# The output projection of six of eight sequences as seven products of 128x128 blocks, its matrix read by groups from memory

## The chip, the core and the metric

The program runs on one core of a Trainium2 chip, alone. The metric is device time in microseconds (us). Names used below: PE is the matrix engine (its weight loads, which run beside the products, are listed as PEld), DVE the vector engine, ACT the scalar engine, POOL the GpSimd engine, SP the engine that only issues transfers. A transfer (DMA) is issued by SP, ACT or POOL and carried out by sixteen DMA engines that all of them share. SBUF is the memory that the engines work on, PSUM the one that PE writes to; both have 128 partitions.

## What is computed

One transformer block over 8 sequences of 512 rows, 256 wide: attention with 16 query heads in 4 groups (each group has one key and one value head), then a mixture of 64 experts (six for each row) with a shared expert. Cut to what matters here:

```python
q = (x @ wq + bq).reshape(b, t, G, QPG, D).transpose(0, 2, 3, 1, 4)   # G=4 groups, QPG=4 heads each, D=128
k, v = (kv[..., :D], kv[..., D:])
scores = einsum('bgqtd,bgksd->bgqts', q + pe, k + pe) / sqrt(D)       # causal, softmax -> probs
out = einsum('bgqts,bgksd->btgqd', probs, v).reshape(b, t, G * QPG * D)
return out @ wo                                                       # 512 x 2048 times 2048 x 256 per sequence
...
x = x + layernorm(attention(layernorm(x)))
x = x + layernorm(experts(layernorm(x)))
```

The change is about the line `out @ wo`. All data are float32.

## The kernel before

The order of all instructions on every engine is written out by hand; nothing is moved by a scheduler. One loop runs over k = 0 .. 127: eight sequences b, sixteen steps s in each (k = 16 b + s). A step has one quarter of the rows of one group of heads: `scores(k, q)` for four q (products `psc`, L507; DVE masks them and takes the least, L511; ACT takes the exponential, L515), `weigh(k)` (POOL divides by the sum, tile `e`, L525), `turned(k)` (DVE turns 32x32 blocks into `eb`, L543; SP writes `eb` to memory `ex_d` in four transfers, L547, and reads it back as `et` in one, L553) and `mix(k)` (products `pav` of `et` with the values, L580; ACT adds a bias and leaves the result `ao`, L591). They are staggered: step k of the loop holds `scores(k)`, `weigh(k)`, `turned(k - 1)` and `mix(k - 2)`. A step's data therefore leave SBUF and come back while PE works on the two following steps, and this order, together with the one queue of SP, sets when `et` is there.

Two steps make a half j = k // 2 of a group: four heads, two row tiles of 128. `project(j, i)` multiplies one tile's four heads with the group's 4 x 128 rows of `wo` into one PSUM bank pair `po` (tags o0 and o1), which adds up over the four groups of a sequence. It runs two halves later: `projections(k)` handles half k // 2 - 2, one tile in the even step and the other in the odd one. The whole matrix, `wo_sb` (2 MB), stays in SBUF. After a sequence's last half ACT copies the sums out (`copies`, L1026), in step s = 2 of the next sequence; layer norm, gate and experts of that sequence follow in later steps (`feed_forward`, places such as "5B" or "6M" in the step).

Where DVE, ACT or POOL have work of a sequence's feed forward, steps are longer; a step takes 6.2 to 9 us where there is little of it (s = 14, 15, 0 to 5), about 8 to 14 us elsewhere, and 14 to 23 us late in the run, where the experts' weights are loaded (ACT's queue) and multiplied.

The queries are already made in a similar way: `ask` and `answer` (L411) form each pair of heads from seven products of summed blocks instead of eight.

Of the kernel before, what the change touches and what calls it, by code (L numbers as in the profile page):

```python
# [19 lines left out]
P = 128  # L20
B, T, E = 8, 512, 256
NT = B * T
NI = T // P
# [18 lines left out]
LROW = ROW + NX  # L42
TH = T // 2
JOINED_FROM, JOINED_TO = 2, (EARLY + 1) * G

@with_exitstack
def sandwich_kernel(ctx, tc, x, wq, bq_t, wkv, bk_t, bv, wo, gate_wt, w_gate, w_up, w_down,
# [19 lines left out]
    y_d = dram.tile([2 * (ET_ROWS + CAP), E], F32, tag="y_d", name="y_d")  # L67
    lxg_d = dram.tile([NT - ET_ROWS, LROW], F32, tag="lxg_d", name="lxg_d")
    ly_d = dram.tile([NT - ET_ROWS, E], F32, tag="ly_d", name="ly_d")

    def bank(shape, name):
        return ps_m.tile(shape, F32, tag="m", name=name)
# [80 lines left out]
    with ExitStack() as part:  # L153
# [13 lines left out]
        def load(ap, shape, name):  # L167
            t = wpool.tile(shape, F32, tag=name, name=name)
            nc.sync.dma_start(out=t, in_=ap)
            return t  # L170
# [18 lines left out]
        for c in range(NC):  # L189
# [6 lines left out]
        bv_sb = load(bv.rearrange("(g d) -> d g", d=D), [D, G], "bv_sb")  # L196
        wq_sb = [wq_first] + [load(wq[:, ts(g, QPG * D)].rearrange("(c p) n -> p c n", p=P), [P, NC, QPG * D],
                                   f"wq_sb{g}") for g in range(1, G)]
        wo_sb = load(wo.rearrange("(h d) e -> d h e", d=D), [D, NH, E], "wo_sb")

        sg_sb, su_sb = [wpool.tile([P, NC, FSH + NX // 2], F32, tag=name, name=name) for name in ("sg_sb", "su_sb")]
        for half, (t, w) in enumerate(((sg_sb, sh_gate_t), (su_sb, sh_up_t))):
# [315 lines left out]
        def weigh(k):  # L518
            l = live[k]
            recip = small.tile([P, NI], F32, tag="recip", name=f"recip_{k}")  # L520
            nc.vector.reciprocal(recip, l["total"])  # L521
            engine = nc.gpsimd if k < NK - 1 else nc.vector
            for q in range(NI):
                e = blocks_of(k, q)
                engine.tensor_scalar(e, e, recip[:, q : q + 1], 1.0, ALU.mult, ALU.mult)  # L525
# [45 lines left out]
        def mix(k):  # L571
            b, g, m, _ = units_of(k)
            et = live.pop(k)["et"]

            pav = [bank([P, QPG, 2, HALF], f"pav_{k}")] * 2
            if k == NK - 1:
                pav[1] = bank([P, QPG, 2, HALF], f"pav_{k}_1")
            for n, _, first, count in placed(k):
                for j in range(count):
                    nc.tensor.matmul(pav[n // NI][:, :, n % 2, :], lhsT=seqs[b]["v"][g][:, j, :], rhs=et[:, :, first + j, :],  # L580
                                     start=j == 0, stop=j == count - 1, skip_group_check=True)
            if k % 2 == 0:
                results[k // 2] = {i: p2.tile([D, QPG, P], F32, tag="ao", name=f"ao_{k}_{i}", bufs=3)
                                   for i in tiles_at(k // 2)}
            bias = bv_sb[:, g : g + 1]
            for n, _, _, _ in placed(k):
                ao = results[k // 2][n // 2][:, :, ts(n % 2, HALF)]
                if k == NK - 1 and n < NI:
                    nc.vector.tensor_scalar_add(ao, pav[n // NI][:, :, n % 2, :], bias)
                else:  # L590
                    nc.scalar.activation(ao, pav[n // NI][:, :, n % 2, :], AF.Identity, bias=bias)  # L591
# [3 lines left out]
        def tiles_at(j):  # L595

            return (1, 2) if j % 2 else (0, 3)

        def project(j, i):
            b, n = divmod(j, 2 * G)  # L600
            if n == 0 and i == 0:
                po[b] = [ps_o.tile([P, 2, E], F32, tag=f"o{n}", name=f"po_{b}_{n}") for n in range(2)]
            ao = results[j].pop(i)
            for h in range(QPG):
                nc.tensor.matmul(po[b][i // 2][:, i % 2, :], lhsT=ao[:, h, :], rhs=wo_sb[:, n // 2 * QPG + h, :],  # L605
                                 start=n == 0 and h == 0, stop=n // 2 == G - 1 and h == QPG - 1, skip_group_check=True)

        def projections(k):

            j, odd = divmod(k, 2)  # L610
            j -= 2
            if j < 0:
                return
            if j % (2 * G) == 2 * G - 1:
                tiles = () if odd else tiles_at(j)
            else:
                tiles = tiles_at(j)[odd : odd + 1]
            for i in tiles:
                project(j, i)

# [394 lines left out]
        def feed_forward(b):  # L1017


            xt, sums = seqs[b]["x"], po.pop(b)  # L1020
            l = {}

            def copies():
                l["o"] = p1.tile([P, NI, E], F32, tag="xn", name=f"o_{b}")
                for n in range(2):
                    nc.scalar.copy(l["o"][:, ts(n, 2), :], sums[n])  # L1026
# [223 lines left out]
        queries(1)  # L1250
        values(0, 0, 0)
        values(0, 0, 1)
        behind, ahead = {}, iter(())
        routed, zeroing = experts(), zeros()
        twice, finishing = False, 0
        FIRST_FREE = (EARLY + 1) * NH + 6
# [4 lines left out]
        for k in range(NK):  # L1261
# [7 lines left out]
            if s == 6 and b <= EARLY:  # L1269
                ahead = prepare(b + 1)  # L1270
                next_rows.append(next(ahead))
            if 0 <= k - 1 < NK - 2:
                turned(k - 1)
            if twice and not finishing:
# [14 lines left out]
            if k < 2:  # L1289
                queries(k + 2)  # L1290
            weigh(k)
            if b <= EARLY and s == 7:
                next(ahead)()
            side(s, "A")
# [23 lines left out]
            if k == 2:  # L1318
                group_step(2)
                group_step(3)  # L1320
            if k >= 2:
                mix(k - 2)
            if in_pairs(k - 1):
# [20 lines left out]
                load_down("late")  # L1344
            if s == 2 and b:
                behind = feed_forward(b - 1)
            side(s, "D")
            if s == 6 and b == EARLY + 1:
                ahead = prepare(b + 1)
# [108 lines left out]
```

## Time and profile before

| | |
|---|---|
| median of three runs | 1357.95 us (1354.87 to 1360.82) |
| time of the profiled execution | 1357.09 us |
| its span, first to last instruction | 1355.4 us |
| instructions | 20372 |
| PE, PEld | 98 %, 75 % of the span |
| DVE, ACT, POOL | 65 %, 40 %, 34 % |
| granted PE clock | 0.996 |
| DMA | 261.32 MB, mean 193 GB/s |

A share is busy time over the span. Durations of products in the profile overlap, since products are pipelined: what a product costs PE is the distance from its start to the next one's start, read from a timeline. A float32 product shows as two rows (two instructions), so that `project` has 1024 rows for 512 products. A transfer's row gives only the time that its engine needs to issue it; when it landed is seen from who waits for it.

### The profile page before, as it was taken

Reading aid. Unit: us, or ns where it says so; the run is one execution under the profiler, and the core shown is the slowest. Engines: PE = TensorE matmul, PEld = TensorE weight load, DVE = VectorE, ACT = ScalarE, POOL = GpSimd, SP = SyncE. Lnnn points to the kernel's source line nnn. Section 1 sums busy time; section 2 is a strip of 40 time slices with the busy share of each in tenths; the row PEclk is TensorE's granted clock in tenths of the full one; section 3 lists DMA queues with packets and bytes.
Section 4 is the critical chain, followed back from the end, with each engine's and each line's share of the span. In section 5 each row is a group of like instructions: output and inputs, shape, how many; then the busy total and the mean of one; then the engine's idle time right before and its main releaser. Section 6 shows DMA issues by size and latency. Waiting matters only on the chain. (4 is left out here: it accounts for less than half of the span.)

```text
span 1355.4 us, 20372 instructions
## 1 busy us (share of the span) xinstructions
PE 1333.5 (98%) x6266; PEld 1015.5 (75%) x6266; DVE 879.9 (65%) x2871; ACT 543.7 (40%) x1655; POOL 460.8 (34%) x772
## 2 busy tenths in 40 slices
PE   9999999999999999999999999999999999999997
PEld 6888777788778887788778877876666766767774
DVE  5575577766776677667786678657666444567545
ACT  3343354334443444334433443334433343434423
POOL 4334232313231242223221232134554444445511
PEclk9999999999999999999999999999999999999999
DMA  8676667655674576466665556569998889777712
GB/s 266 175 201 172 192 195 207 158 154 159 209 186 132 151 218 189 118 171 174 201 166 152 156 171 183 151 194 292 304 268 258 244 255 291 182 238 227 244 36 71
DMA packets 167388, 261.32 MB, mean 193 GB/s; under 512 B 17756, under 2 KB 141629, under 8 KB 167277
## 3 DMA queue, kind: packets, MB, share of 16 engines
q1 hardware_dynamic: 129117, 206.76, 52.9%
q10 hardware_dynamic: 32016, 43.78, 10.4%
q0 software_dynamic: 6144, 9.44, 3.6%
q8 instruction: 51, 0.84, 0.3%
q14 instruction: 60, 0.49, 0.1%
HBM read 147.99 MB, written 111.94 MB: 192 GB/s over the span
## 5 line engine op out<-in xcount | busy, mean ns | idle before, releaser
L525 POOL TENSOR_SCALAR e<-e,recip 128x512 f32<-128x512 f32 (+1 forms) x504 | 245.8, 527 | 684.2 <-DVE recip L521 543.2
L515 ACT ACTIVATE e<-e,least 128x32 f32<-128x32 f32 (+1 forms) x504 | 259.4, 517 | 259.2 <-DVE least L511 242.6
L580 PE MATMUL pav<-et,v 128*128 128x256 f32 x1280 | 301.5, 383 | 8.4 <-DMA et<-ex_d 7.6
L580 PEld LDWEIGHTS pav<-et,v 128*128 128x128 f32 x1280 | 243.2, 191 | 48.4 <-DMA et<-ex_d 7.5
L511 DVE CUSTOM_DVE_ANT_0 e<-psc,mask 128x32 f32<-128x32 f32 (+1 forms) x504 | 203.8, 430 | 111.7 <-PE psc L507 109.7
L507 PE MATMUL psc<-kt,qt 128*128 128x32 f32 (+15 forms) x1024 | 275.5, 407 | 0.8 <-DVE qt L372 0.4
L591 ACT ACTIVATE ao<-pav,bv_sb 128x256 f32<-128x256 f32 x255 | 107.2, 471 | 379.3 <-PE pav L580 356.5
L605 PE MATMUL po<-wo_sb,ao 128*128 128x256 f32 x1024 | 241.9, 380 | 0.0
L605 PEld LDWEIGHTS po<-wo_sb,ao 128*128 128x128 f32 x1024 | 193.3, 190 | 51.3 <-issue 16.6
L507 PEld LDWEIGHTS psc<-kt,qt 128*128 128x128 f32 x1024 | 161.1, 191 | 60.4 <-DVE least L511 26.0
L543 DVE STREAM_TRANSPOSE eb<-e 128x1024 f32<-128x1024 f32 (+1 forms) x252 | 197.5, 822 | 2.1 <-POOL e L525 1.5
L515 ACT ACTIVATION_READ_ACCUMULATOR e<-e,least 128x1 f32 x504 | 95.5, 190 | 0.0
L848 POOL DMA_INDIRECT y_d<-dd,idx x32 | 50.9, 1589 | 91.2 <-DMA y_d<-dd,idx 27.0
L367 PE MATMUL pq<-xnt,wq_sb 128*128 128x256 f32 x320 | 75.5, 380 | 0.2 <-DMA wq_sb<-in_wq 0.2
L320 DVE SCALAR_TENSOR_TENSOR kt<-pk,bk_sb,pe_sb 128x512 f32<-128x512 f32 x32 | 24.0, 750 | 76.6 <-PE pk L318 73.9
L411 PE MATMUL pq_back<-rows_joined,heads 128*128 128x256 f32 x264 | 71.3, 379 | 0.0
L329 PEld LDWEIGHTS pv<-wkv_sb,xnt 128*128 128x128 f32 x512 | 65.9, 192 | 4.5 <-issue 1.1
L329 PE MATMUL pv<-wkv_sb,xnt 128*128 128x128 f32 x512 | 67.5, 275 | 0.5 <-ACT ao L591 0.5
L367 PEld LDWEIGHTS pq<-xnt,wq_sb 128*128 128x128 f32 x320 | 59.5, 190 | 9.8 <-DMA wq_sb<-in_wq 1.1
L411 PEld LDWEIGHTS pq_back<-rows_joined,heads 128*128 128x128 f32 x264 | 50.2, 190 | 16.2 <-issue 8.2
L318 PE MATMUL pk<-xnt,wkv_sb 128*128 128x512 f32 x128 | 60.5, 595 | 0.4 <-DMA wkv_sb<-in_wkv 0.4
L120 DVE COPY ht<-pth 88x256 f32<-88x256 f32 x32 | 13.4, 419 | 63.3 <-PE pth L828 58.5
(237 smaller groups left out, 1534.4 us busy)
## 6 DMA issues: line engine op xcount, KB each, us to landing
ex_d<-eb SPq DMA_DIRECT2D x504, 160.0 KB
et<-ex_d SPq DMA_DIRECT2D x126, 640.0 KB
wgu<-in_w_gate ACTq DMA_DIRECT2D x32, 352.0 KB
wgu<-in_w_up ACTq DMA_DIRECT2D x32, 352.0 KB
wd<-in_w_down ACTq DMA_DIRECT2D x32, 352.0 KB
y<-y_d ACTq DMA_DIRECT2D x10, 512.0 KB
x<-in_x SPq DMA_DIRECT2D x7, 512.0 KB
out_dram<-x SPq DMA_DIRECT2D x7, 512.0 KB
```

Of the source, the lines that this page charges most:

```text
L318: nc.tensor.matmul(pk, lhsT=wkv_sb[:, c, g, 0, :], rhs=s["xnt"][:, c, :], start=c == 0, stop=c == NC - 1)
L329: nc.tensor.matmul(pv[:, i, :], lhsT=s["xnt"][:, c, ts(2 * n + i, P)], rhs=wkv_sb[:, c, g, 1, :], start=c == 0, stop=c == NC - 1, skip_gro ...
L367: nc.tensor.matmul(pq[:, n, :, :], lhsT=wq_sb[g][:, c, ts(2 * pair + n, D)], rhs=seqs[b]["xnt"][:, c, :].rearrange("p (u v) -> p u v", v=P ...
L411: nc.tensor.matmul(out, lhsT=factor[0], rhs=factor[1], start=first, stop=last, skip_group_check=True)
L507: nc.tensor.matmul(psc[:, :w], lhsT=halves[k // 2][:, at, :, :].rearrange("d h t -> d (h t)"), rhs=seqs[b]["kt"][g][:, :w], start=True, st ...
L511: nc.vector.tensor_tensor_reduce(out=e, in0=psc[:, :w].rearrange("p (c t) -> p c t", t=BS), in1=mask[:, T - w :].rearrange("p (c t) -> p c ...
L515: nc.scalar.activation(e, e, AF.Exp, bias=l["least"][:, q : q + 1], scale=-1.0, accum_out=l["total"][:, q : q + 1])
L525: engine.tensor_scalar(e, e, recip[:, q : q + 1], 1.0, ALU.mult, ALU.mult)
L543: nc.vector.transpose(eb[:, :, first : first + count, :, :].rearrange("p a j r t -> p j a r t"), weighed[k % 2][:, end - count : end, :, : ...
L580: nc.tensor.matmul(pav[n // NI][:, :, n % 2, :], lhsT=seqs[b]["v"][g][:, j, :], rhs=et[:, :, first + j, :], start=j == 0, stop=j == count ...
L591: nc.scalar.activation(ao, pav[n // NI][:, :, n % 2, :], AF.Identity, bias=bias)
L605: nc.tensor.matmul(po[b][i // 2][:, i % 2, :], lhsT=ao[:, h, :], rhs=wo_sb[:, n // 2 * QPG + h, :], start=n == 0 and h == 0, stop=n // 2 = ...
```

## The change

For sequences 1 to 6 (`CROSSED`) the projection of one half, a 2 x 2 problem of blocks (two row tiles, two pairs of heads, two halves of the 256 columns, each block pair twice for n = 0, 1), is made from seven products of blocks instead of eight. PE has 14 products of 128x128x128 per half instead of 8 of 128x128x256.

- `cross(j)` forms four sums of blocks of `ao` on POOL, at the head of the even step. `straight(j)` (6 products, bank o0) stands in the even step, `across(j)` (8 products, bank o1) in the odd one; for the last half of a sequence both are in the even step.
- The banks no longer add up over the groups. `add_up` adds each bank to `partial` in SBUF: ACT copies it for the first two halves, DVE adds it (`tensor_add`) for the other six. `combine` (POOL, six instructions) makes the two row tiles' outputs from the seven sums, twice a sequence; ACT's `copies` goes.
- `wo_sb` goes. `load_whole(n)` reads one group's 512 KB in ACT's queue (sequences 0 and 7, and the first in the prologue). While sequence 0 is worked on, `make_sets` forms each group's seven blocks on POOL and writes them to memory; in sequences 1 to 6 `load_sets` reads them back in ACT's queue, 384 KB (`ws`) in steps with k % 4 = 3 and 512 KB (`wc`) in steps with k % 4 = 0, one buffer each, after the exponentials of that step.
- `ao` has one buffer of both tiles instead of three of one tile, so ACT may write the next half only when `cross` and `straight` have read the last. In sequences 0 and 7 both tiles are projected in the even step.

```diff
+CROSSED = range(1, B - 1)
-        wo_sb = load(wo.rearrange("(h d) e -> d h e", d=D), [D, NH, E], "wo_sb")
+        def load_whole(n):
+            t = whole[n] = wpool.tile([D, QPG, E], F32, tag="wc", name=f"wo_{n}")
+            nc.scalar.dma_start(out=t, in_=wo.rearrange("(h d) e -> d h e", d=D)[:, ts(n % G, QPG), :])
+        load_whole(0)
+        partial = wpool.tile([P, 2, 7, P], F32, tag="partial", name="partial")
...
+        def make_sets(g):
+            w = blocks_of_whole(whole[g])
+            t = p1.tile([P, 4, 2, P], F32, tag="xt2", name=f"sets_{g}")
+            for k in range(2):
+                nc.scalar.dma_start(out=ws_d[g][:, k], in_=w[:, k, 0])
+            nc.scalar.dma_start(out=wc_d[g][:, 0], in_=w[:, 1, 1])
+            nc.gpsimd.tensor_sub(t[:, 0], w[:, 0, 1], w[:, 0, 0])
+            nc.gpsimd.tensor_sub(t[:, 1], w[:, 1, 1], t[:, 0])
+            yield
+            nc.gpsimd.tensor_sub(t[:, 2], w[:, 1, 1], w[:, 0, 1])
+            nc.gpsimd.tensor_sub(t[:, 3], w[:, 1, 0], t[:, 1])
+            yield
+            nc.scalar.dma_start(out=wc_d[g][:, 1:], in_=t[:, :3])
+            nc.scalar.dma_start(out=ws_d[g][:, 2], in_=t[:, 3])
+            yield
+        def load_set(n, d, name):
+            t = wpool.tile(list(d[0].shape), F32, tag=name, name=f"{name}_{n}")
+            nc.scalar.dma_start(out=t.rearrange("p k n e -> p (k n e)"), in_=d[n % G].rearrange("p k n e -> p (k n e)"))
+        def cross(j):
+            x11, x12, x21, x22 = sides_of_results(j)
+            t = crossed[j] = p2.tile([D, 4, 2, P], F32, tag="ac", name=f"crossed_{j}", bufs=1)
+            nc.gpsimd.tensor_add(t[:, 1], x21, x22)
+            nc.gpsimd.tensor_sub(t[:, 2], t[:, 1], x11)
+            nc.gpsimd.tensor_sub(t[:, 3], x11, x21)
+            nc.gpsimd.tensor_sub(t[:, 0], x12, t[:, 2])
+        def straight(j):
+            x11, x12, _, x22 = sides_of_results(j)
+            w = sets[j // 2]["ws"]
+            po[j, 0] = multiply(j, [[(x[:, n], w[:, k, n]) for k, x in enumerate((x11, x12, x22))] for n in range(2)],
+                                "ps", "o0")
+        def across(j):
+            w, t = sets[j // 2]["wc"], crossed.pop(j)
+            po[j, 1] = multiply(j, [[(t[:, k, n], w[:, k, n]) for k in range(4)] for n in range(2)], "pc", "o1")
+        def add_up(j, part):
+            ...
+            if n < 2:
+                on_act(sums, bank_)
+            else:
+                nc.vector.tensor_add(sums, bank_, sums)
+        def combine(b, odd):
+            ...
+            nc.gpsimd.tensor_add(first[:, 0], t[:, 0], t[:, 1])
+            nc.gpsimd.tensor_add(t[:, 5], t[:, 0], t[:, 5])
+            nc.gpsimd.tensor_add(t[:, 6], t[:, 5], t[:, 6])
+            nc.gpsimd.tensor_add(t[:, 3], t[:, 4], t[:, 3])
+            nc.gpsimd.tensor_add(second, t[:, 2:5:2], t[:, 6:7].to_broadcast([P, 2, P]))
+            nc.gpsimd.tensor_add(first[:, 1], t[:, 5], t[:, 3])
...
             if k % 2 == 0:
-                results[k // 2] = {i: p2.tile([D, QPG, P], F32, tag="ao", name=f"ao_{k}_{i}", bufs=3)
-                                   for i in tiles_at(k // 2)}
+                tag = "ac" if b == B - 1 and k % 4 else "ao"
+                results[k // 2] = p2.tile([D, 2, QPG, P], F32, tag=tag, name=f"ao_{k}", bufs=1)
...
             scores(k, 3)
             scores(k, 2)
+            projections_before(k)
...
             weigh(k)
+            load_sets(k)
...
+            projections_behind(k)
...
             if s == 2 and b:
                 behind = feed_forward(b - 1)
+            projections_end(k)
+            if k % NI == 0 and 1 <= k // NI <= G:
+                making = make_sets(k // NI - 1)
+            next(making, None)
+            if k % NI == 2 and k // NI and k // NH not in CROSSED:
+                load_whole(k // NI)
```

## The prediction

> **What bounds the kernel now.** I read the page first, then the timeline of PE, the list of waits, and the timeline of all engines in a stretch of short steps. On the page PE is busy all the time, and the two groups that matter here are the projection (L605, 256 columns) and the one group of products with 128 columns and full weights (L329):
>
> ```profile
> PE 1333.5 (98%) x6266; PEld 1015.5 (75%) x6266; DVE 879.9 (65%) x2871; ACT 543.7 (40%) x1655; POOL 460.8 (34%) x772
> ...
> L605 PE MATMUL po<-wo_sb,ao 128*128 128x256 f32 x1024 | 241.9, 380 | 0.0
> ...
> L329 PE MATMUL pv<-wkv_sb,xnt 128*128 128x128 f32 x512 | 67.5, 275 | 0.5 <-ACT ao L591 0.5
> ```
>
> The means (380 and 275 ns) overlap. The price is the distance of starts, from PE's timeline: eight rows of 128 columns take 622.97 - 622.08 = 0.89 us, 111 ns each; eight of 256 take 626.81 - 625.08 = 1.73 us, 216 ns each.
>
> ```profile
> 622.08 1.05 PE L329 MATMUL pv<-wkv_sb,xnt 128*128 128x128 f32 x8
> 622.97 2.27 PE L507 MATMUL psc<-kt,qt 128*128 128x32 f32 x8
> 625.08 1.89 PE L605 MATMUL po<-wo_sb,ao 128*128 128x256 f32 x8
> 626.81 1.03 PE L411 MATMUL pq_front<-xnt,wq_sb 128*128 128x256 f32 x4
> ```
>
> So PE is bound by the sum of such distances, with hardly a wait. The largest that the list of waits has for PE is the data that came back from memory:
>
> ```profile
> PE pav L580 <- DMA et<-ex_d: 7.6, 7, 2.4
> ```
>
> That it is small does not mean it is far away. In short steps the way out and back just fits. Step 67, from the timeline of all engines (writes of step 66's data, the step's last exponential, the read back, its first use):
>
> ```profile
> 619.74 1.85 SPq L547 DMA_DIRECT2D ex_d<-eb  x4
> ...
> 621.10 0.19 ACT L515 ACTIVATION_READ_ACCUMULATOR e<-e,least 128x1 f32 x1
> ...
> 624.09 0.34 SPq L553 DMA_DIRECT2D et<-ex_d  x1
> ...
> 628.53 2.39 PE L580 MATMUL pav<-et,v 128*128 128x256 f32 x10
> ```
>
> Issue to use is 4.44 us. How much of it is needed shows where PE's weight load did wait for it, 3.97 us after the issue:
>
> ```profile
> 301.16 0.34 SPq L553 DMA_DIRECT2D et<-ex_d  x1
> ...
> 305.13 0.94 PEld L580 LDWEIGHTS pav<-et,v 128*128 128x128 f32 x5 [0.30 <-DMA et<-ex_d]
> ```
>
> So the margin of step 66 is 4.44 - 3.97 = 0.47 us, that of step 31 (the lines above) is none. Read in the same way over sequences 1 to 4, steps s = 2, 3, 15 have 0 to 1.6 us, steps s = 6 to 12 about 2.4 to 10 us. So there are two regimes: in long steps PE alone decides, in short ones PE and the exchange are level.
>
> **The gain.** Per half, 16 rows at 216 ns (3.46 us) become 28 at 112 ns (3.14 us; 111 or 112 ns, I take the dearer). Over 6 sequences of 8 halves: 768 x 0.216 = 165.9 us against 1344 x 0.112 = 150.5 us, 15.4 us less on the bound engine. The even step loses 0.40 us, the odd one gains 0.05. Sequences 0 and 7 keep their products.
>
> [...]
>
> **Work on other engines that I cost at nothing, and its cover.**
>
> ```profile
> 587.01 1.90 POOL L525 TENSOR_SCALAR e<-e,recip 128x320 f32<-128x320 f32 x4 [5.29 <-DVE recip L521]
> ...
> 590.39 0.19 DVE L511 CUSTOM_DVE_ANT_0 e<-psc,mask 128x32 f32<-128x32 f32 x1 [3.14 <-PE psc L507]
> ...
> 596.35 1.89 POOL L525 TENSOR_SCALAR e<-e,recip 128x512 f32<-128x512 f32 x4 [7.43 <-DVE recip L521]
> ...
> 598.16 0.26 DVE L511 CUSTOM_DVE_ANT_0 e<-psc,mask 128x96 f32<-128x96 f32 x1 [1.54 <-PE psc L507]
> ```
>
> `cross`: four POOL adds of 128x256. L1040 has two in 1.42 us (631.13), so 2.8 us per half, 136 us in all. It stands behind the `e` work that ends at 588.9, waits for `ao` until 589.8 and is done at 592.6; the next `e` work comes at 596.35, so 3.7 us of idle time remain. Queued behind it: ACT's next `ao`, which waits for `cross` now that `ao` has one buffer, at 597.97, 5 us later. `combine` (six, the widest 0.71, so under 4 us) comes in steps 1 and 2, behind `e`. If these covers were gone, each us on POOL would go into the exchange, whose turning on DVE waits for `e`.
>
> `add_up`: 36 halves on DVE. L456 takes 0.42 us for 256 columns out of PSUM, so about 0.55 and 0.70 for 384 and 512. DVE's idle time before a step's first masking is 3.14 us after an odd step, 1.54 after an even one. The other 12 halves go to ACT (0.53 us for 512 columns, L1026), whose idle time before `ao` is mostly over 2 us. A set load costs ACT about 0.37 us of issue (L1043), with `ao` behind it, which waits for PE anyway. If DVE's cover were gone, its turning, and with it the writes, would be late by the excess.
>
> **Where time is lost.** The margin of each read shrinks by 0.35 us, as the two steps that it spans get shorter; and transfers are added, 48 set loads, 8 loads of whole groups and 20 writes of sets. What a transfer in the way costs is seen in step 53, against a step with nothing in the way:
>
> ```profile
> 484.80 1.86 SPq L547 DMA_DIRECT2D ex_d<-eb  x4
> 485.90 0.37 ACTq L1043 DMA_DIRECT2D x_d<-x  x1
> ...
> 491.04 0.34 SPq L553 DMA_DIRECT2D et<-ex_d  x1
> ```
>
> ```profile
> 592.45 2.04 SPq L547 DMA_DIRECT2D ex_d<-eb  x4
> ...
> 596.72 0.34 SPq L553 DMA_DIRECT2D et<-ex_d  x1
> ```
>
> With 512 KB issued between the writes, first write to read takes 6.24 us, else 4.27: 1.97 us. A set load is issued after the step's last exponential: 621.29 in step 67, 1.55 us after the first write, when the fourth is being issued, so most of it should go behind the writes and into the 1 us or so before the read's data move. Bounds for one load: 0 and 1.97 us (1.5 for 384 KB); I take 0.2, nearest to the clean row, since the row in the way was issued 0.45 us earlier.
>
> [...]
>
> The terms, each with its bounds:
> - Set `ws` in s = 3, the shortest step (6.2 us): issued 621.29, needed by `straight` at 625.08, 3.79 us. A read of 640 KB needs 3.97; this one has 384 KB but starts behind the writes, which land by 624.09. Between 0 and 1.4 us; I take 0.5, which also covers the lost margin of steps 2 and 3, because PE's wait there gives the read that time. Six times: 3.0 us (0 to 8).
> - The other tight places, mainly s = 14 to 0: 0.15 us a sequence, 0.9 us (0 to 12, the top with 1.97 us at s = 15).
> - Sequence 0, no gain there: at the ends of steps 6, 10 and 14 about 1 MB goes out ahead of the next step's writes. Up to 3.9 us each; margins are 0.9, 0.9 and 2.4 us (issue to use 77.3 to 82.2, 110.3 to 115.2, 142.2 to 148.6). I take 2.0 us of 0 to 7.
> - Sequence 7: of four loads of 512 KB three stand before an exchange, where reads are already late:
>
> ```profile
> 1267.92 3.95 PE L580 MATMUL pav<-et,v 128*128 128x256 f32 x10 [2.01 <-DMA et<-ex_d]
> ```
>
>   I take 1.5 us of 0 to 6. The 2 MB that no longer come first shorten nothing, as no product waits for them: 0.
> - Late in the run (904 to 1190 us) DMA is 91 % busy, but the margins there are mostly 4 to 18 us: 0.
>
> Sum: -15.4 + 3.0 + 0.9 + 2.0 + 1.5 = -8.0 us. The profiled execution took 1357.09 us (span 1355.4 and 1.7 around it), 0.9 below the median of 1357.95; so 1349.1 for such an execution, and 1350.0 as a median.
>
> **Rivals.**
> 1. Everything is hidden: -15.4 and about 0.5 for margins that are already zero, 1343. For it: PE's rows have no idle time in most stretches. Against: step 31 has no margin at all.
> 2. Slower: the set loads are served among the writes and not behind them. Then each exchange of a step with a load is late by the load's own length, 1.5 or 2 us. In a sequence s = 2 costs 1.5 + 0.35 - 0.47 = 1.4 us, s = 15 costs 2.0 + 0.35 less a margin of about 1, 1.3 us, and s = 3 with s = 14 about 0.7 between them: 3.4 a sequence, 20 in six; sequences 0 and 7 at 2.3 and 2.7: in all 25, net +9, 1367. It decides from about 1.2 us per load; below that the gain covers it. For it: step 53. Against: the later issue.
> 3. In between, 0.6 to 1.2 us per load, or a DVE or POOL cover that gives out now and then: 9 to 22 us lost, within 0.5 % of before, about 1355.
> 4. Products of 128 columns do not stream at 112 ns when their moving side is a set: from 123 ns on the gain is gone. The rows of L329 speak against it.
>
> **How the numbers follow.** A median under 1351.2 is faster by over 0.5 %, which is about what a measurement of this kernel can tell from no change; over 1364.7 is slower by as much. My forecast 0.35 and rival 1 at 0.15 make faster 0.50. Rival 3 makes same 0.22. Rival 2 at 0.25 and rival 4 at 0.03 make slower 0.28. The range goes from rival 1 (1342) to rival 2's value (1367), with about 2 in 10 outside, nearly all above; the forecast's own range is 1344 to 1352.
>
> **What would show it.** PE's projection rows at 111 to 112 ns, 1344 of them. PE's wait for `et` up from 7.6 us to some 15 in all, at s = 2, 3 and 15, in sequence 0 and in sequence 7. A small wait before `straight` in s = 4. First write to read near 4.3 us in steps with k % 4 = 3 or 0; 5.5 us or more there means rival 2. POOL 48 % busy and DVE 68 %, with idle time left before `e` and before the first masking. I am wrong if PE waits in long steps, or if DVE or POOL takes the place of the transfer as the one waited for.

## The result and the profile after

| | before | changed |
|---|---|---|
| median | 1356.78 us (1353.82 to 1360.82, 5 runs) | 1400.65 us (1399.14 to 1407.79, 5 runs) |
| time, span of the profiled execution | 1357.09, 1355.4 us | 1402.70, 1400.9 us |
| granted PE clock | 0.996 | 0.990 |

The ratio is 1.033 with a 95 % interval of 1.030 to 1.037: slower by 44 us, where 8 us of gain were forecast, and 34 us above the top of the range. The first two fences are the page of the changed kernel, busy time and groups:

```profile
PE 1333.5 (95%) x6842; PEld 1024.3 (73%) x6842; DVE 917.1 (65%) x2943; ACT 548.4 (39%) x1667; POOL 641.2 (46%) x1052
```

```profile
L666 PE MATMUL pc<-wc,crossed 128*128 128x128 f32 x768 | 94.5, 276 | 0.8 <-POOL crossed L660 0.8
...
L666 PE MATMUL ps<-ws,ao 128*128 128x128 f32 x576 | 72.3, 275 | 0.3 <-DMA ws<-ws_d 0.3
```

PE is busy 95 % of a longer span and not 98 %: it waits. It hardly waits for what the change adds (0.8 us for the crossed sums, 0.3 us for a set). The list of waits of the changed kernel says for what (in total, times, longest):

```profile
PE pav L591 <- DMA et<-ex_d: 39.9, 26, 3.5
PE psg L1094 <- DMA xt<-exr_d: 6.9, 4, 2.1
PE psc L518 <- DVE least L522: 2.2, 5, 0.8
```

The wait for the probabilities that went out and came back was 7.6 us and is 39.9. The second line was not there before at all: `exr_d` is the same kind of exchange for the rows of the feed forward (L143 and L145, also in SP's queue), needed in step s = 8. The timeline of the changed kernel over one stretch of short steps, SP's and ACT's queues and PE (start, duration):

```profile
649.91 1.90 SPq L558 DMA_DIRECT2D ex_d<-eb  x4
...
650.69 0.36 ACTq L644 DMA_DIRECT2D ws<-ws_d  x1
...
656.16 0.34 SPq L564 DMA_DIRECT2D et<-ex_d  x1
...
656.60 2.31 SPq L558 DMA_DIRECT2D ex_d<-eb  x4
...
656.77 0.33 ACTq L644 DMA_DIRECT2D wc<-wc_d  x1
...
660.92 2.40 PE L591 MATMUL pav<-et,v 128*128 128x256 f32 x10 [1.94 <-DMA et<-ex_d]
...
664.11 0.34 SPq L564 DMA_DIRECT2D et<-ex_d  x1
```

First write to read is 656.16 - 649.91 = 6.25 us in the first exchange and 7.51 in the second; it was 4.27 where nothing stood in the way. The second is longer: its load is larger, `wc` comes 0.17 us after the first write, and its writes stand in SP's queue directly behind a read that is already late.

Read over all steps 25 to 88, the medians of first write to read (us) are as follows; `ws` is loaded in the steps of the first column, `wc` in those of the second. The last column is what PE's steps took more (+) or less (-) than before (start of a step's first scores to the next step's), summed over three stretches of the loop, in the profiled executions.

| kernel | k % 4 = 3 | k % 4 = 0 | steps 0-23 / 24-95 / 96-124 |
|---|---|---|---|
| before | 4.48 | 4.81 | |
| changed | 6.52 | 7.23 | +9.9 / +27.6 / +6.7 |
| e1, no set loads | 4.47 | 4.60 | +9.0 / -8.2 / -3.0 |
| e2, before and reads | 6.59 | 7.46 | +8.4 / +29.9 / -3.3 |
| e4, no sums | 6.64 | 7.29 | +11.3 / +19.4 / +6.1 |
| e5, parts in SP's queue | 4.81 | 5.04 | +7.0 / -3.4 / +8.7 |
| e6, rows of 1 KB | 6.45 | 7.43 | +9.2 / +30.0 / -0.7 |
| e12, behind ao | 5.28 | 6.33 | +15.9 / +16.2 / +3.1 |

Each row is one execution, and one execution can be off by some 6 us in the last column. e11 and e6, described below, carry the changed kernel's loads at the changed kernel's places; they read +22.1 and +30.0 in the second stretch, +1.9 and -0.7 in the third. e13 and e15, whose instructions are the same up to step 28, read +4.5 and +10.7 in the first.

By place in the sequence (mean of steps 24 to 87) the changed kernel loses 2.8 us in s = 8, 2.2 in s = 4, 1.4 in s = 5 and 1.2 in s = 1; the other steps stand within 0.6 us of before.

In s = 7 and 11 the exchange is late for a second reason, and the loss in s = 8 comes from it. The list of waits has it for SP's queue, and the timeline shows one case (step 39, s = 7):

```profile
SPq L558 <- DMA ws<-ws_d: 42.9, 9, 6.5
```

```profile
373.02 6.99 SPq L558 DMA_DIRECT2D ex_d<-eb  x4
...
373.86 0.33 ACTq L644 DMA_DIRECT2D ws<-ws_d  x1
...
380.12 0.38 SPq L145 DMA_DIRECT2D xt<-exr_d  x1
...
385.12 1.95 PE L1094 MATMUL psg<-xt,sg_sb 128*128 128x512 f32 x4 [1.46 <-DMA xt<-exr_d]
```

The four writes take 6.99 us to issue and not 1.9. In the changed kernel's trace the transfers of SP's and of ACT's queue name the same eight semaphores, numbers 100 to 107. The second write waits for number 100 and updates it, and the `ws` load of 373.86 updates it too; the load's last update, its landing, comes at 378.73, and the write goes out at 378.74. So SP's whole queue stood still here until a load of another queue had landed (5.4 us by the list of waits), and the read of `xt` behind it, at 380.12, is late too. From step 23 to 91 the trace has the same, a write that waits for the semaphore of a set load, behind nine of the `ws` loads and four of the `wc` loads (s = 8), never in the other places. No run changes the semaphores alone, so what this costs in all is not measured.

### The profile page after: what moved, and what is told of

Same layout as the page of the kernel before. It is cut to its first block, busy times and chain, and to the rows that moved or that the text cites. A ratio compares the mean times of both kernels' runs of the same rounds, so it can differ in the third digit from the quotient of the medians.

```text
span 1400.9 us, 22036 instructions
## 1 busy us (share of the span) xinstructions
PE 1333.5 (95%) x6842; PEld 1024.3 (73%) x6842; DVE 917.1 (65%) x2943; ACT 548.4 (39%) x1667; POOL 641.2 (46%) x1052
## 3 DMA queue, kind: packets, MB, share of 16 engines
q10 hardware_dynamic: 47568, 73.67, 16.3%
## 5 line engine op out<-in xcount | busy, mean ns | idle before, releaser
L591 PE MATMUL pav<-et,v 128*128 128x256 f32 x1280 | 307.9, 389 | 41.6 <-DMA et<-ex_d 39.9
L666 PEld LDWEIGHTS pc<-wc,crossed 128*128 128x128 f32 x768 | 92.5, 192 | 7.8 <-issue 4.3
L666 PE MATMUL pc<-wc,crossed 128*128 128x128 f32 x768 | 94.5, 276 | 0.8 <-POOL crossed L660 0.8
L666 PEld LDWEIGHTS ps<-ws,ao 128*128 128x128 f32 x576 | 71.6, 192 | 18.2 <-issue 8.4
L971 POOL DMA_INDIRECT y_d<-dd,idx x32 | 50.8, 1588 | 66.7 <-DMA y_d<-dd,idx 22.1
L666 PE MATMUL ps<-ws,ao 128*128 128x128 f32 x576 | 72.3, 275 | 0.3 <-DMA ws<-ws_d 0.3
L422 PEld LDWEIGHTS pq_back<-rows_joined,heads 128*128 128x128 f32 x264 | 50.2, 190 | 16.2 <-issue 8.2
```

The lines of the kernel that those rows point to most:

```text
L422: nc.tensor.matmul(out, lhsT=factor[0], rhs=factor[1], start=first, stop=last, skip_group_check=True)
L666: nc.tensor.matmul(bank_[:, n, :], lhsT=a, rhs=w, start=pair == 0 and n == 0, stop=pair == 1 and n == len(factors[0]) - 1, skip_group_chec ...
L971: nc.gpsimd.indirect_dma_start(out=y_d[:, :], out_offset=bass.IndirectOffsetOnAxis(ap=table["idx"][:, m, 1:2], axis=0), in_=pairs.pop(m)[" ...
```

## The experiments

Theory A: the set loads in ACT's queue delay the exchange, and PE waits for it where steps are short. Theory B: the added work on POOL and DVE, or the single `ao` buffer, does it. Edits are shown in part (`...`); each is against the kernel that the text names, else against the changed one.

### Loads taken away, loads added alone, sums taken away, loads moved

**e1_no_set_loads**

```diff
-            if step == 3 and (n // G) in CROSSED:
+            if step == 3 and n == G:
                 load_set(n, ws_d, "ws")
-            if step == 0 and n and (n - 1) // G in CROSSED:
+            if step == 0 and n == G + 1:
                 load_set(n - 1, wc_d, "wc")
+                for other in range(G + 1, (B - 1) * G):
+                    sets[other] = sets[G]
```

> The set loads of sequences 1 to 6 are left out but for the first group's, whose blocks serve all groups (so the projection's values are those of another matrix); sequence 0's forming and writing of sets, cross, add_up and combine all stay. Theory A (the set loads get in among the exchange's writes, the read of et is issued late, PE waits for it in short steps): first write to read falls back to about 4.3 us in the steps that had a load, PE's wait for et falls from 39.9 us to about 10, and the time to about 1353 us (1348 to 1358); what stays over 1342 is sequence 0 and 7. Theory B (POOL's cross in front of the e work, DVE's add_up in front of the masking, the single ao buffer): the time stays at 1395 us or more, since all of that is still there.

1360.29 us, ratio 1.004 (1.002 to 1.006). PE's waits:

```profile
PE pav L591 <- DMA et<-ex_d: 14.3, 10, 3.0
PE psc L518 <- DVE least L522: 2.2, 5, 0.8
```

40 of the 44 us are the set loads', and theory B falls already here: the sums, the additions and the single `ao` buffer are all still in this kernel. In steps 24 to 95 the gain is there at last, 8.2 of 11.9 us. The wait for `xt<-exr_d` is gone too. But the time is not below before: sequence 0 still costs 9 us, and the median lies 4 us above the profiled execution (1356.17), at a lower clock (a median of 0.994 over its runs against 0.997 for before).

**e2_before_and_reads**

The reads are added to the kernel before:

```diff
+            if 7 <= k < 7 + G:
+                nc.scalar.dma_start(out=wog_d[k - 7], in_=rows_of_group(k - 7, QPG))
+            if step == 3 and 0 < n // G < B - 1:
+                nc.scalar.dma_start(out=rows_of_group(n + 2, 3), in_=wog_d[(n + 2) % G][:, : 3 * E])
+            if step == 0 and n and 0 < (n - 1) // G < B - 1:
+                nc.scalar.dma_start(out=rows_of_group(n + 1, QPG), in_=wog_d[(n + 1) % G])
```

> The kernel before, with 48 reads added in ACT's queue at the very places of the change (384 KB at k % 4 = 3, 512 KB at k % 4 = 0, sequences 1 to 6, whole rows of 3 or 4 KB per partition), from a copy of the matrix that four writes at k = 7 to 10 leave in memory, into rows of wo_sb that are not used until eight steps later. So nobody waits for them, the values stay the same, and products, POOL and DVE are as before. Theory A: slower by 30 to 50 us, 1387 to 1407, with first write to read at 5.5 to 8 us in those steps; less than the change lost, as steps are not shortened here. Theory B: 1357 to 1362. If only the waits of straight and across for their sets mattered, and not the exchange, it would also be 1357 to 1362.

1399.8 us, ratio 1.033 (1.030 to 1.035): as much as the change loses in all, by reads that nobody waits for (and four writes of 512 KB in sequence 0 that prepare them), in a kernel without any of its products or sums. SP's queue is held here as well, 51.5 us in 13 waits, so e2 does not tell the two reasons apart. The waits, and one exchange of the timeline with 384 KB in the way (646.61 to 651.94, 5.33 us):

```profile
PE pav L584 <- DMA et<-ex_d: 35.8, 23, 2.8
```

```profile
646.61 1.89 SPq L551 DMA_DIRECT2D ex_d<-eb  x4
...
647.39 0.35 ACTq L1264 DMA_DIRECT2D wo_sb<-wog_d  x1
...
651.94 0.34 SPq L557 DMA_DIRECT2D et<-ex_d  x1
```

**e4_no_sums**

```diff
+            if j % (2 * G):
+                crossed[j] = crossed[j - 1]
+                return
...
-            else:
-                nc.vector.tensor_add(sums, bank_, sums)
```

> The changed kernel with all loads in their places in ACT's queue, but cross is done only for the first half of each sequence (its sums serve the other seven), and DVE's add_up is left out (only the first two halves are added up), so the projection's values are wrong. Theory A: 1390 to 1402 us, first write to read in steps with a load as in the changed kernel, PE's wait for et near 40 us. Theory B: down to about 1350, with PE's wait for et below 12 us.

1400.93 us, ratio 1.034 (1.030 to 1.039). With 37 % of POOL busy and not 46 %, and no `add_up` on DVE, nothing is won. (The single `ao` buffer is still there; e1 answers for that.)

```profile
PE pav L591 <- DMA et<-ex_d: 40.8, 26, 5.1
```

**e3_sp_in_parts**

```diff
+SLOTS = {"ws": ((2, 1), (2, 1), (3, 0)), "wc": ((3, 1), (4, 0), (4, 1), (4, 1))}
...
-            nc.scalar.dma_start(out=t.rearrange("p k n e -> p (k n e)"), in_=d[n % G].rearrange("p k n e -> p (k n e)"))
+            for k, at in enumerate(SLOTS[name]):
+                put(n * NI + at[0], at[1], t[:, k], d[n % G][:, k])
```

The other loads and the writes of sets of sequences 0 and 7 move in the same way. (`put` hands a block to SP's queue in a step, 0: behind the four writes, 1: behind the read.)

> The changed kernel, whole and with the same bytes, but every set load, every load of a whole group after the first and every write of sets goes out in SP's queue in parts of 128 KB (one of 384), placed behind the four writes of an exchange (ahead of its read) or behind the read, never ahead of writes of the same step. Theory A, when order in the queue is what matters: first write to read back near 4.3 us, 1343 to 1352 us, faster than before. Theory A, when it is the bytes themselves that the exchange cannot bear wherever they stand: 1370 to 1395. Theory B: 1395 or more.

1437.84 us, ratio 1.060 (1.056 to 1.063): slowest of all, and for another reason. Its waits:

```profile
PE pc L681 <- DMA wc<-wc_d: 44.0, 21, 8.4
PE po L629 <- DMA wo<-in_wo: 23.7, 7, 5.6
PE pav L604 <- DMA et<-ex_d: 7.6, 6, 2.9
```

The exchange is on time as in the kernel before (7.6 us). What stands behind the read in one queue is now late itself. I had not costed that.

### Order, row size, place

**e5_sp_earlier**, against e3:

```diff
-SLOTS = {"ws": ((2, 1), (2, 1), (3, 0)), "wc": ((3, 1), (4, 0), (4, 1), (4, 1))}
+SLOTS = {"ws": ((2, 1), (2, 1), (3, 0)), "wc": ((3, 1), (3, 1), (4, 0), (4, 0))}
```

> As e3_sp_in_parts, where the exchange was on time (PE waited 7.6 us for et) but the sets were late (PE waited 44.0 us for wc): the same parts, now at most 256 KB to a place and one place earlier, so that the last part of a set stands behind the writes of the step before its use, and never behind that step's read. Theory A (order in the queues): the wait for wc goes and the wait for et stays below 15 us, 1345 to 1356. If two parts of 128 KB behind the writes hold up the read of et, or the parts behind the read hold up the next writes, as much as the loads in ACT's queue did: 1375 to 1400, with first write to read over 5.5 us in nearly every step.

1372.1 us, ratio 1.010 (1.007 to 1.014). The same bytes, 28 us less than the changed kernel. So the bytes alone are not what costs. But e5 changes several things at once: the queue, the place in it, the size of the parts, and with the queue the transfers that SP's writes wait for. From step 24 to 87 no set load holds the exchange's writes any more, and s = 8, the place that hung on it, is 2.8 us a sequence shorter than in the changed kernel, of 7.7 for all places. How much of the rest is the place in the queue and how much the smaller parts, no run tells. What remains is s = 4 and 5, sequence 0, and the stretch where the experts' weights are loaded (+8.7 us from step 96 on, worse than in ACT's queue).

```profile
PE pav L604 <- DMA et<-ex_d: 23.0, 18, 4.2
```

**e6_rows_of_1k**

```diff
-            nc.scalar.dma_start(out=t.rearrange("p k n e -> p (k n e)"), in_=d[n % G].rearrange("p k n e -> p (k n e)"))
+            nc.scalar.dma_start(out=t.rearrange("p k n e -> p k (n e)"), in_=d[n % G].rearrange("(k p) f -> p k f", p=P))
...
```

> The changed kernel with the same loads in the same places of ACT's queue, but the sets lie in memory block by block, so a load is 384 or 512 rows of 1 KB and not 128 rows of 3 or 4 KB. The exchange's writes are rows of 1280 B. [...] Theory A2 (a load that is issued first is served first, or bytes share evenly): no change, 1395 to 1405.

1398.67 us, ratio 1.032 (1.025 to 1.038), first write to read as in the changed kernel, as A2 has it, and for which of its two reasons the run does not tell: no effect of the length of the load's rows is seen, also not in the places where SP's queue is not held. (In the changed kernel's trace a packet of 4 KB has a median of 159 ns on a DMA engine, one of 1280 B 55 and one of 1 KB 46.)

**e12_behind_ao**

```diff
-            if step == 3 and (n // G) in CROSSED:
+            if step == 2 and (n // G) in CROSSED:
                 load_set(n, ws_d, "ws")
-            if step == 0 and n and (n - 1) // G in CROSSED:
-                load_set(n - 1, wc_d, "wc")
+            if step == 3 and (n // G) in CROSSED:
+                load_set(n, wc_d, "wc")
...
             projections_end(k)
+            load_sets(k)
```

> The changed kernel, the same loads whole and in ACT's queue, but issued at the end of a step, behind that step's ao, and so behind the exchange's writes and the issue of its read (ws at the end of k % 4 = 2, wc at the end of k % 4 = 3, as early as the buffers allow). It tries the step of the prediction that the load goes for little once it is issued behind the writes. If that is so: first write to read falls to about 4.5 us, 1360 to 1378 us. If a whole load is in the way wherever it stands, now of the read's data and of the next writes: 1385 to 1405, with issue of read to its landing over 4.5 us or first write to read again over 5.5 us.

1387.33 us, ratio 1.022 (1.017 to 1.026), 13 us less than the changed kernel. First write to read is 1 us better, but from the start of the read's issue to its landing, a median of 3.95 us before and 4.70 in the changed kernel for k % 4 = 3 (steps 25 to 88), it takes 5.95 here:

```profile
PE pav L591 <- DMA et<-ex_d: 33.9, 20, 4.7
```

So a whole load is in the way in both places that were tried; behind the writes `wc` delays the read's data.

### What is lost without set loads

**e7_no_other_sets_made**

```diff
-            if k % NI == 0 and 1 <= k // NI <= G:
+            if k % NI == 0 and k // NI == 1:
                 making = make_sets(k // NI - 1)
```

> As e1_no_set_loads (1360 us), and only the first group's set is formed and written in sequence 0; the loads of whole groups stay (projection's values wrong as there). e1 still lost 9 us up to step 24. If these come from writing the sets (1 MB in front of the next step's writes, and POOL's subtractions in front of e): 1351 to 1355, most of it gained in steps 8 to 21. If they come from the loads of whole groups in sequence 0: 1358 to 1361.

1357.08 us, ratio 1.002 (0.999 to 1.004); +6.0 us up to step 24, against e1's +9.0. Neither of the two cases that I had set up: both are part of it.

**e8_add_later** (against e5), the wait in s = 13 that DVE's `add_up` makes: 0.35 us on PE, a step that is 0.46 us longer than its products make it. e1, DVE's and PE's timelines:

```profile
268.92 0.55 DVE L686 TENSOR_TENSOR partial<-ps,partial 128x384 f32<-128x384 f32 x1
269.38 0.48 DVE L754 MAX8 sorting<-sorting 128x8 f32<-128x320 f32 x1
...
271.49 0.25 DVE L522 CUSTOM_DVE_ANT_0 e<-psc,mask 128x96 f32<-128x96 f32 x1
```

```profile
271.80 1.02 PE L518 MATMUL psc<-kt,qt 128*128 128x448 f32 x2 [0.35 <-DVE least L522]
```

`add_up` and the router's sorting stand one behind the other, and the masking comes after both.

```diff
-                    add_up(j, 0)
+                    if k % NH != 12:
+                        add_up(j, 0)
...
             weigh(k)
+            if s == 13 and b in CROSSED:
+                add_up((k - 1) // 2 - 2, 0)
```

> As e5_sp_earlier, and DVE's add_up of step s = 12 stands behind the next step's masking instead of in front of the sorting of the router: in e1_no_set_loads PE waited 0.51 us for the masking there in every sequence. Theory: 2.5 to 3 us less than e5_sp_earlier, all in step 29 and its like. If the wait only moves on (to the turning of step 29's data): no change.

1372.17 us: no change from e5. In the profiled execution step 29 did get 0.47 us shorter (14.67 to 14.20), and step 31 was 1.3 us longer; that the exchange takes back what the cover gives is one reading of this single execution, and e15 below does not repeat it.

**e9_both_queues** and **e10_five**, the attempts at a version that beats both kernels:

```diff
+            if n // G == B - 2:
+                nc.scalar.dma_start(out=t.rearrange("p k n e -> p (k n e)"),
+                                    in_=d[n % G].rearrange("p k n e -> p (k n e)"))
+            else:
+                for k, at in enumerate(SLOTS[name]):
+                    put(n * NI + at[0], at[1], t[:, k], d[n % G][:, k])
...
+        for n in range(G):
+            load_whole(n)
```

and e10 against e9:

```diff
-CROSSED = range(1, B - 1)
+CROSSED = range(1, B - 2)
...
```

> The parts in SP's queue of e5_sp_earlier for sequences 1 to 5; for sequence 6, where the experts' weights fill the DMA, the sets whole in ACT's queue where the change has them; and sequence 0's four groups of rows read in the prologue into tiles that sequence 0 has no other use for (wc, ac, partial, xt2), so that no load of a whole group is left in sequence 0. By the steps of the earlier runs against before: sequence 0 some +3 us (the writing of sets), sequences 1 to 5 -3.4 (e5), sequences 6 and 7 +6.6 (the changed kernel): 1362 us, 1354 to 1366. A wait that I have not seen would show as more than 1370.

> As e9_both_queues, but only sequences 1 to 5 are projected with seven products; sequence 6 has the old eight and one load of 512 KB a group, in ACT's queue, in place of 896 KB. Gives up 2.6 us of gain; if it is the bytes of the sets that cost sequence 6 its 5 us, some 2 to 4 us less than e9_both_queues (1351 to 1362); if not, 2 to 3 us more.

1376.3 us, ratio 1.014 (1.011 to 1.018), and 1375.61 us, 1.013 (1.010 to 1.016): neither beats the kernel before, and they do not differ. Some 8 us were a fault of mine (first scores at 24.87 us and not 16.84), seen in e9's list of waits: the four loads of the prologue stood in ACT's queue in front of its first copies. The rest of the distance to the expected 1362 us is not explained.

```profile
PE pk L336 <- ACT xnt L121: 5.6, 1, 5.6
```

**e11_rows_ahead** (the changed kernel with that prologue), **e13_one_set_rows_ahead** (e7 with it), **e14_sets_made_rows_ahead** (e1 with it) and **e15_add_later_too** (e13 and the later `add_up`) have the same late start, so their times tell little:

```diff
-        load_whole(0)
+        for n in range(G):
+            load_whole(n)
...
-            if k % NI == 2 and k // NI and k // NH not in CROSSED:
+            if k % NI == 2 and k // NH == B - 1:
                 load_whole(k // NI)
```

> The changed kernel with one thing altered: sequence 0's four groups of rows are read in the prologue (as in e9_both_queues), so its loads of whole groups go; forming and writing the sets stays, all in ACT's queue. The changed kernel lost 9.9 us up to step 24, e7_no_other_sets_made, with only one group's sets written, still 6. If the loads of whole groups are the larger part: 5 to 7 us less than the changed kernel, 1394 to 1396, with a loss up to step 24 of 3 to 5 us. If not: 1399 to 1401.

> As e7_no_other_sets_made (1357 us: no set loads but the first group's, one set formed and written), and sequence 0's groups of rows are read in the prologue, so that nothing of the change's traffic is left in sequence 0 but one set's writes. Projection's values wrong as there. If the loads of whole groups cause what sequence 0 still loses (6 us up to step 24): 1349 to 1352, loss up to step 24 below 2 us. If sequence 0 loses by its own order (both tiles in the even step, longer even and shorter odd steps): 1356 to 1358.

> As e13_one_set_rows_ahead, but all four sets are formed on POOL and written in ACT's queue in sequence 0. If forming and writing costs what the step from e1 (1360 us) to e7 (1357 us) suggested: 3 us more than e13_one_set_rows_ahead; if it is loads and writes together that were too much: about the same as e13_one_set_rows_ahead.

> As e13_one_set_rows_ahead, and add_up of step s = 12 behind the next step's masking, as in e8_add_later, now with no set loads that could take back what is gained: PE's wait of 0.51 us at s = 13 goes, 2 to 2.5 us less than e13_one_set_rows_ahead, and with that 1346 to 1350: the gain that the prediction's sum had, when nothing is loaded. If the wait moves on to the exchange of that step: no change.

1406.65, 1363.04, 1367.05 and 1362.21 us (ratios 1.039, 1.005, 1.008, 1.003). In e15 step 29 is 0.47 us shorter than in e13, as in e8, and steps 24 to 95 are 1.7 us shorter (-8.5 against -6.8), where four such steps make 1.9; the medians, of 12 runs each that scatter by 5 to 8 us either way, are too coarse to show it.

**e16_one_set_rows_in_sp** and **e17_sets_made_rows_in_sp** are e13 and e14 with the start put right (the edit is against these):

```diff
-            nc.scalar.dma_start(out=t, in_=wo.rearrange("(h d) e -> d h e", d=D)[:, ts(n % G, QPG), :])
+            (nc.sync if n < G else nc.scalar).dma_start(out=t, in_=wo.rearrange("(h d) e -> d h e", d=D)[:, ts(n % G, QPG), :])
```

> As e13_one_set_rows_ahead, with the four loads of the prologue in SP's queue, where the kernel before reads its matrix. In e13_one_set_rows_ahead they stood in ACT's queue and held up the start: the first scores came at 24.09 us and not at 16.84, and that hid what the loop gained (steps 0 to 125 took 1247.3 us against 1255.2). If that is all: the first scores at about 17 us, 1355 to 1357 us as a median against 1363, faster than before in the profiled execution by some 7 us, and with it the loads of whole groups in sequence 0 shown to cost 3 to 5 us against e7_no_other_sets_made.

> As e16_one_set_rows_in_sp, but all four sets are formed and written in sequence 0 (e14_sets_made_rows_ahead with its start put right). 4 us more than e16_one_set_rows_in_sp, as e14 was over e13, if the forming and writing of the sets is what costs sequence 0 the rest; the same if it was the late start.

1355.68 us, ratio 1.001 (0.999 to 1.003), and 1358.62 us, 1.002 (1.000 to 1.004). The late start is gone (first scores at 16.3 and 16.4 us), and e16's profiled execution is 5 us faster than before's, but its median is not; that execution is the fastest of its 12, and before's lies 1.8 us above the median of 1355.32 measured beside it. Forming and writing three more sets costs sequence 0 about 3 to 4 us: three pairs of medians say so (e7 to e1 3.2, e13 to e14 4.0, e16 to e17 2.9). No cost of the loads of whole groups is seen (e7 1.002, e16 1.001), where I expected 3 to 5 us. Up to step 24 the two profiled executions lose 4.8 and 8.7 us, which fits but is within the scatter of one execution. Of the 4.8 us of e16, 3.2 fall in step 20, behind the one set load that these kernels keep:

```profile
174.45 1.91 SPq L563 DMA_DIRECT2D ex_d<-eb  x4
...
175.31 0.36 ACTq L650 DMA_DIRECT2D ws<-ws_d  x1
...
185.38 4.08 PE L596 MATMUL pav<-et,v 128*128 128x256 f32 x10 [2.32 <-DMA et<-ex_d]
```

PE waits 2.32 us, and the ten products behind the wait take 4.08 us and not 2.40.

## Why the prediction was wrong

**Right: products and sums.** Eight or six products of 128 columns start 111 to 112 ns apart (from the timeline, `pc` x16 in 1.78 us), undisturbed even steps are 0.39 us shorter and odd ones 0.06 longer: 48 x 0.33 = 15.8 us against the 15.4 of the sum. Rival 4 is out. POOL's and DVE's added work costs nothing that is seen but DVE's cover below (e4), and the single `ao` buffer nothing (e1, where the undisturbed steps have their full gain).

**Wrong: the value of 0.2 us per set load.** That step failed. Measured by the table, 384 KB cost 6.52 - 4.48 = 2.0 us and 512 KB 7.23 - 4.81 = 2.4 us, above even the upper bounds of 1.5 and 1.97. These medians mix two things. Where the load is only in the way of the exchange's data, first write to read is longer by 1.1 us in s = 3, 2.0 in s = 15 and 2.6 to 2.9 in s = 0, 4 and 12 (medians of steps 24 to 95 by place); where SP's queue also waits for the load to land, by 4.8 us in s = 7 and 2.9 in s = 11. The second was in neither the sum nor a rival. Both halves of the reason for 0.2 were wrong:
- *"A set load is issued after the step's last exponential."* I took the place behind the step's last exponential for the time of issue. In the changed kernel's timeline the load leaves 0.78 us after the first write (649.91, 650.69), median 0.84 over the 24 loads of `ws` and 1.18 over those of `wc`: before the last exponential has run, and about when the store in step 53 left (1.10) from which I took the upper bound, not 0.45 us later. By my own rule, to take the nearest row, the upper bound was the value.
- *"So most of it should go behind the writes."* e12 puts it there, and it is in the way of the read's data instead. No run found a free place for a whole load in an exchange; e5, which does better, has them in parts of 128 KB.

**Wrong: the count of places.** Rival 2 had the right mechanism and the right sign, but 3.4 us a sequence. From steps 24 to 95 (4.5 sequences) the changed kernel lost 27.6 + 11.9 of gain = 39.5 us, 8.8 a sequence. What rival 2 left out: (1) the two loads stand in consecutive exchanges, and SP's one queue hands the delay on, as the next writes stand behind the late read; (2) I took s = 6 to 12 as safe by their margins of 2.4 us and more and did not price s = 4 and 5, where the feed forward's own loads and stores stand too, and where PE now waits (347.03 and 355.85 in the last section); (3) the holding of SP's queue in s = 7, and through it the other exchange, `exr_d`, which s = 8 waits for (6.9 us): I read the waits of before for what was large there, and this one was zero. The term for the `ws` load's own reader, 3.0 us, was too high: `straight` waits 0.3 us for it in the whole run. For "Late in the run: 0" the profiles differ: in steps 96 to 103 the changed kernel loses 5.2 us, but e6 and e11, with the same loads there, -0.5 and 1.3, so that it failed is not shown.

**Wrong: sequence 0 at 2.0 us.** Up to step 24 it costs 9 to 10 us (e1 and the changed kernel), above the bound of 7, in executions that scatter by some 6 us there. Making and writing three of the four sets is 3 to 4 of it (the pairs of medians above), and what the sum had not is that these writes, in ACT's queue, hold SP's queue too (15.1 us in six waits of SP in the changed kernel: `wc_d<-sets` 9.2, `ws_d<-wo` 5.9). How the rest is divided is not shown. Sequence 7 can't be told apart from the end of sequence 6.

**Wrong, small: DVE's cover.** Idle time before the masking was read where no sorting stands. In s = 13 it gave out by 0.46 us in each of four sequences, 1.9 us in all (four of the five waits in the `least` line; the fifth, of 0.8 us, is late in the run, in s = 10).

**Not counted: the clock after a wait.** See the last section; some 7 us, by an estimate.

So rival 2 is what happened where the load is only in the way, with a median price per load some 20 to 35 % higher, and the holding of SP's queue, which no rival had, came on top; the loss per sequence is 2.6 times what rival 2 gave it. And with all set loads but the first gone (e16) the gain of 15.8 us still does not reach the median. In the profiled execution 5 us are left of it: 5 went up to step 24 and 1.9 at the sorting, the others are small. The median lies 3.6 us above that execution (1352.09), at a clock of 0.9955 against 0.997 for before (medians over the runs); why the clock is lower stays open. No version that beats the kernel before was found.

## What to carry to other kernels

Before you put a transfer of half a megabyte into another queue, look whether a chain "write out, read back, use" runs at its limit on the same DMA engines: there it cost up to its whole length and more here (1.1 to 2.9 us for loads of 1.5 and 2.0, by the prediction's estimate), and SP's queue, which holds both directions, handed the delay on to the next round (the writes of 656.60 behind the late read of 656.16). Look also in the list of waits of the queue itself for transfers of another queue: here SP's stood for 42.9 us, in nine waits, until a `ws` load of ACT's queue had landed, which no transfer of SP reads. Take the time of issue of a planned transfer from a transfer that already stands at that place of its queue, not from the end of the instruction in front of it. And when one wait is priced, list the other exchanges that share its path, also those that do not wait yet.

## What the runs showed of the hardware

A wait of PE cost more than itself in some places of these runs. Three waits in the changed kernel, PE's timeline, and then PE in the two stretches of 3.41 us around the third (columns: us, PE busy and instructions, granted clock, DMA share, GB/s):

```profile
160.59 2.43 PE L591 MATMUL pav<-et,v 128*128 128x256 f32 x10 [2.35 <-DMA et<-ex_d]
...
347.03 2.40 PE L591 MATMUL pav<-et,v 128*128 128x256 f32 x10 [1.84 <-DMA et<-ex_d]
...
355.85 3.59 PE L591 MATMUL pav<-et,v 128*128 128x256 f32 x10 [1.88 <-DMA et<-ex_d]
```

```profile
353.55:356.96 3.41, 1.53 (x7) 1.00 0.99 276
356.96:360.37 3.41, 3.41 (x10) 0.50 0.29 81
```

After the first two the ten products take 2.4 us; behind the third the granted clock falls to 0.50 for 3.41 us (356.96 to 360.37), and they take 3.59. The clock record has six such stretches within the changed kernel's loop (from 189.71, 356.96, 541.28, 814.35, 978.18 and 1237.60) and two within before's (1193.51 and 1268.60). At 0.50 a stretch of 3.41 us does 1.71 us less work: 10.2 us against 3.4, so by this estimate some 7 of the 44 us. The line of step 1267.92 that the prediction quotes (3.95 us for ten products after a wait of 2.01; the clock is 0.50 from 1268.60 to 1272.01) showed it already, and I read only the wait in it.

The length of one wait does not tell whether it comes to that: 1.88 us were followed by half clock here, and 2.35 were not. In the changed kernel the six stretches start whole numbers of 3.41 us apart (49, 54, 80, 48 and 76), and in the 3.41 us ahead of each of them PE is idle for 1.88 to 3.29 us; ahead of before's two it is 2.45 and 2.01. The third wait lies inside such a stretch (353.55 to 356.96). Counted on in the same steps of 3.41 us, the first wait falls across a border, 0.75 us of it in one stretch and 1.60 in the next, and the clock is 1.00 in both and in the one behind them. That is what the two profiles show; what sets the clock they do not.

The other surprise is that the same set loads (48, 22 MB) cost 28 us more or less by the queue, the place and the parts in which they go out (e5 against the changed kernel), and no difference was seen for the length of their rows (e6).
